# Graph layer on one core: the gathered-row step cut into five turns of five fours instead of six of four, with the PSUM banks shared out anew

## The chip, the core and the metric

The kernel runs on one core of one Trainium2 chip. The core has a matmul engine (PE, with its weight loads shown as PEld), a vector engine (DVE), an activation engine (ACT), a general engine (POOL), a queue engine (SP) and 16 DMA engines. PE writes only to PSUM, which has eight banks of 512 fp32 columns for each of 128 partitions; DVE and ACT read PSUM and read and write SBUF. The metric is device time of one execution in microseconds (us), lower being better.

## The reference

There are 12,500 nodes with 128 features and 400,000 edges, sorted by destination, each of one of two types. Every edge takes its source node's row through one of two linear maps, the results are summed at the destination, a self map is added, then relu, the residual and a layer norm:

```python
Xs = X[src]
m_data = Xs @ W_data.T + b_data
m_ctrl = Xs @ W_control.T + b_control
msg = jnp.where((edge_types == 0)[:, None], m_data, m_ctrl)
agg = jax.ops.segment_sum(msg, dst, num_segments=X.shape[0])
out = jax.nn.relu(agg + (X @ W_self.T + b_self))
return _layernorm(X + out)
```

Since the maps are linear, the kernel sums source rows for each destination and type first and multiplies by the weights once per node, in `finish_batch`.

## The kernel before

**Windows.** The edges are cut into 25 groups; a group holds five "p" windows and five "e" windows (the last e window of every odd group is joined to the p window before it). The main loop has 113 steps, one for each e window of 20 columns of 128 edges. A p window has 5 columns (25 where it is joined), which are spread over the steps, some eight columns a step.

**Rows of p windows** are gathered from memory: POOL issues an indirect DMA for each column (`fetch`, L743), and `chunk` sums them with three matmuls for the rows, which are held as three bf16 parts (L694), and one for the counts (L779).

**Rows of e windows** are picked on PE from node rows that stay in SBUF (`x3`). All edges of a window are sorted by source block ("cell") and rank beforehand, and a 0/1 matrix `pick` makes a matmul choose rows. Four cells make a "four", which is one bank of PSUM: four matmuls with 32 columns of weights each, side by side in four lanes of the array (`pick`, L808). There are 24 fours and half a one in a step, and edges that fit in no cell go to the tile `last`, gathered by POOL (L787).

**A step** (`picked`) has units. A unit first picks its fours into PSUM (`rows`, tile `got`), two fours to a tile, and ACT casts each tile of two banks to bf16 in SBUF (L820, tile `emsg`). Then it counts (L832) and adds (L694) the fours of the unit before it: a selection `esel` (edge against destination, made by DVE in `choose`, L500) is multiplied with the messages and summed into a bank of `sums`. The last unit's fours are added in `end`, which runs in the first unit of the next step, and then DVE adds the bank into `acc` (`accumulate`, L732).

**PSUM.** `ps1` has one bank, `side`, used for many short things in turn; `ps2` has three banks for `sums`, which e and p windows share; `psg` has two tiles of two banks for `got`. Together that is eight.

**Ranks for the window two steps on** are worked out in the same step: PE counts who stands ahead (L575, L516), DVE reduces and multiplies (L585 to L600), builds the value matrix (L626), PE puts values into cells (`put`, L638, in `side`), ACT copies them (`spread`, L646), SP writes them to memory and loads them back to all partitions as `pick` (L648, L650), DVE compares (L680), and PE turns the codes (`turn_codes`, L658, from ACT's copy). `O` (L500) and `prod` (L567, L568) of the next window are made in between.

**Order.** The code is recorded in the order in which `merged` sorts units by their place in the step (0 to 1): the units of `picked` lie evenly, the others at places that are written out, and a scheduler then places each engine's instructions by what it takes to be ready. Every engine runs its own queue in that order, and pools of tiles give the waits: a new tile waits until the last reader of the buffer that it takes is done. `paced` ties POOL's gathers to the picks of a unit.

Of the kernel before, what the change touches and what calls it, by code (L numbers as in the profile page):

```python
# [17 lines left out]
P = 128  # L18
D = 128
# [131 lines left out]
def short_path(ctx, tc, const, ident, eps, wT, brow, bad, x, src, dst, etype, ws, bs, out):  # L151
# [9 lines left out]
    ps2 = ctx.enter_context(tc.tile_pool(name="ps2", bufs=3, space=PSUM))  # L161
    psg = ctx.enter_context(tc.tile_pool(name="psg", bufs=2, space=PSUM))
# [379 lines left out]
    def give_slots(w):  # L542
# [39 lines left out]
        def ranks():  # L582
# [10 lines left out]
            half = big.tile([P, EC, h], BF, name="half")  # L593
# [69 lines left out]
        def keep_codes():  # L663
# [128 lines left out]
    def picked(w, tiled, ending, fin_used, before):  # L792
# [5 lines left out]
        per, pair = 4, 2  # L798

        def choose(q0, n=8):  # L800
# [13 lines left out]
        def rows(q):  # L814
            ps = psg.tile([P, pair, 512], FP, name="got")
            msg = two.tile([P, pair, 3 * D], BF, name="emsg", bufs=5)
            for k in range(pair):
                last = pick(ps[:, k, :3 * D], q + k)
                s["msg"][q + k] = msg[:, k, :]
            nc.scalar.copy(msg, ps[:, :, :3 * D])  # L820
            return last

        def last_rows():
            q = NQ - 1
            ps = psg.tile([P, pair, 512], FP, name="got")[:, 0] if fin_used else side()
            pick(ps[:, :3 * D], q, 2)
            nc.scalar.copy(s["msg"][q][OVF:, :], ps[OVF:, :3 * D])
# [13 lines left out]
        def unit(t):  # L841

            if t == 1 and w > 0:
                spare.append(lambda: spare_rows(w))
            for q in range(t * per, (t + 1) * per, pair):
                gate = rows(q)
            paced(w + (t + 1) / turns, gate)
            if t % 2:
                paced(w + (t + 1) / turns, gate)
            else:  # L850
                paced(w + (t - 1.5) / turns, gate)
            if t in (0, 1):
                choose(8 * t)
            if t == 0:
                ending()
            if t == 2:
                assert not spare
                s["msg"][NQ - 1] = slots[w]["last"]
            if t == 3:
                choose(16, 9)  # L860
            if t > 0:
                for q in range((t - 1) * per, t * per if t < turns - 1 else NQ):
                    count(q)
            if t == turns - 2:
                last_rows()
            if t == 1 and before:
                before()
            if t > 0:
                add((t - 1) * per, t * per)
# [12 lines left out]
        turns = (NQ - 1) // per  # L882
# [96 lines left out]
    def last_spares():  # L979
# [7 lines left out]
        return {6: [lambda: None, turn, s[3]]}, [(0.1, s[0]), (0.28, s[1])]  # L987
# [44 lines left out]
    def ending():  # L1032
        pass

    for w in range(pairs):
# [16 lines left out]
        units, ending = picked(w, tiled, ending, bool(rest), begin.pop(0)[1] if begin else None)  # L1052
# [181 lines left out]
```

## Time and profile before

| | before |
|---|---|
| median of 3 runs | 2022.85 us (2015.96 to 2024.19) |
| profiled execution | 2019.71 us, its span 2018.0 us |
| granted TensorE clock, mean | 0.993 |
| PE busy | 1758.2 us, 87% |
| DVE busy | 1654.6 us, 82% |
| ACT busy | 1318.0 us, 65% |
| POOL busy | 1222.2 us, 61% |
| casts of picked rows (L820) | 1356, 800 ns each |
| picks (L808 into `got`) | 10896, from 66.6 to 1993.2 us |

A share of busy time is a mean over stages; the timeline shows start, length, engine, line, operation, the tile written and those read, how many instructions are merged in the row, and in brackets how long the engine was idle before it and what ended that. A row of groups has the count, the total and the mean in ns, then the idle time just before them. A row of waits names who waited for what, with the total, the times and the longest in us. The ends of matmuls in the records are modelled, not observed.

### The profile page before, as it was taken

How to read it: one execution, taken by the hardware profiler on the slowest of the kernel's cores; microseconds unless marked ns; L12 is line 12 of the kernel's file. 1: busy time of each engine (PE TensorE's matmuls, PEld its weight loads, DVE VectorE, ACT ScalarE, POOL GpSimd, SP SyncE). 2: the span in 40 equal slices, each digit the busy share in tenths (PEclk: the TensorE clock that was granted, in tenths of full speed). 3: DMA queues.
4: the chain of work that ended last, by engine and by line, in shares of the span. 5: the costliest groups of instructions: out<-in, count | busy, mean ns of one | idle time of the engine just before them, and what ended most of it. 6: DMA issues, size and time to landing. Idle time of an engine off the chain costs nothing.

```text
span 2018.0 us, 74125 instructions
## 1 busy us (share of the span) xinstructions
PE 1758.2 (87%) x30869; PEld 1352.0 (67%) x30869; DVE 1654.6 (82%) x4158; ACT 1318.0 (65%) x2577; POOL 1222.2 (61%) x995
## 2 busy tenths in 40 slices
PE   0688899899889898999998999988998898999996
PEld 0466677677667676766776776766777677776675
DVE  7978888788788787888888888888888888788872
ACT  4656666676666665666666676666666666666665
POOL 0466666666666656666666666656666666666660
PEclk9999999999999999999999999999999999999999
DMA  8644343343343343443443443443434334334331
GB/s 237 202 115 137 108 140 119 120 134 121 110 138 121 118 138 98 140 135 104 140 122 118 139 123 119 137 124 113 134 124 129 115 122 125 122 125 126 120 101 40
DMA packets 186525, 254.84 MB, mean 126 GB/s; under 512 B 85369, under 2 KB 152995, under 8 KB 183108
## 3 DMA queue, kind: packets, MB, share of 16 engines
q1 hardware_dynamic: 128418, 152.97, 23.2%
q0 software_dynamic: 45136, 90.65, 16.5%
q10 hardware_dynamic: 12626, 6.40, 1.1%
q8 instruction: 243, 3.98, 0.8%
q14 instruction: 102, 0.84, 0.1%
HBM read 231.89 MB, written 18.04 MB: 124 GB/s over the span
## 4 chain that ended last, share of the span: by engine, by line
PE 67%; ACT 11%; DVE 8%; issue 6%; DMA 5%; SPq 1%; another core or an unknown queue 1%; DVEq 0%; ACTq 0%
PE sums L694 28%; PE got L808 25%; ACT emsg L820 8%; DMA pick<-there 3%; PE side L638 3%; PE side L938 3%; PE sums L832 2%; PE side L808 2%; PE side L575 1%; DVE esel L500 1%; PE side L526 1%; PE sums L779 1%; PE side L658 1%; DVE prod L567 1%
## 5 line engine op out<-in xcount | busy, mean ns | idle before, releaser
L743 POOL DMA_INDIRECT msg<-rows,pidx x865 | 1107.8, 1281 | 516.4 <-PE got L808 315.8
L820 ACT CAST emsg<-got 128x768 bf16<-128x768 f32 x1356 | 1025.0, 800 | 380.4 <-PE got L808 236.4
L694 PE MATMUL sums<-esel,emsg 128*128 128x176 bf16 x8136 | 748.9, 240 | 7.6 <-issue 7.2
L808 PE MATMUL got<-x,pick 128*32 128x384 bf16 x10896 | 655.0, 331 | 111.9 <-ACT emsg L820 55.0
L694 PEld LDWEIGHTS <-emsg 128*128 128x128 bf16 x8136 | 593.1, 98 | 121.0 <-issue 101.3
L808 PEld LDWEIGHTS <-pick 128*32 128x32 bf16 x11074 | 260.2, 95 | 291.6 <-issue 190.5
L500 DVE TENSOR_TENSOR esel<-code_col,code 128x1408 bf16<-128x1408 bf16 x339 | 309.1, 912 | 17.6 <-PE sums L694 11.2
L787 POOL DMA_INDIRECT last<-rows,idx x113 | 110.7, 979 | 248.0 <-ACT emsg L820 150.8
L500 DVE TENSOR_TENSOR O<-cell_col,blk 128x2000 bf16<-128x2000 bf16 x113 | 135.4, 1198 | 139.8 <-PE got L808 115.6
L694 PE MATMUL sums<-psel,msg 128*128 128x48 bf16 x2595 | 182.7, 184 | 5.6 <-issue 4.8
L832 PE MATMUL sums<-esel,one_col 128*32 128x176 bf16 x2825 | 166.8, 240 | 6.1 <-DVE esel L500 3.6
L732 DVE TENSOR_TENSOR acc<-acc,sums 128x352 f32 (+2 forms) x238 | 101.8, 428 | 66.5 <-PE sums L694 32.6
L694 PEld LDWEIGHTS <-msg 128*128 128x128 bf16 x2595 | 146.3, 98 | 7.0 <-issue 6.9
L680 DVE TENSOR_SCALAR pick<-pick,lane_f 128x3200 bf16<-128x3200 bf16 x113 | 119.2, 1055 | 32.7 <-DMA pick<-there 27.1
L779 PE MATMUL sums<-psel,one_col 128*128 128x48 bf16 x865 | 144.5, 183 | 1.4 <-issue 1.2
L589 DVE TENSOR_TENSOR prod<-O,ahead 128x2000 bf16<-128x2000 bf16 x113 | 134.4, 1190 | 0.0
L638 PE MATMUL side<-rv,O 128*128 128x64 bf16 x2260 | 91.0, 195 | 34.6 <-DVE rv L626 29.5
L832 PEld LDWEIGHTS <-one_col 128*32 128x32 bf16 x2825 | 85.9, 97 | 44.2 <-issue 9.9
L638 PEld LDWEIGHTS <-O 128*128 128x128 bf16 x2260 | 83.8, 100 | 37.6 <-DVE rv L626 30.2
L646 ACT CAST cell<-side 128x64 bf16<-128x64 f32 x113 | 23.5, 208 | 114.5 <-PE got L808 89.3
L585 DVE TENSOR_REDUCE ahead<-side 128x100 bf16<-128x500 f32 x113 | 76.3, 675 | 23.7 <-PE side L516 20.3
L626 DVE TENSOR_TENSOR rv<-rm,vals 128x1280 bf16<-128x1280 bf16 x113 | 92.2, 816 | 0.1
(172 smaller groups left out, 2008.8 us busy)
## 6 DMA issues: line engine op xcount, KB each, us to landing
pick<-there SPq DMA_DIRECT2D x113, 800.0 KB
acc<-acc_start SPq DMA_DIRECT2D x23, 1280.0 KB
msg<-rows,pidx POOLq DMA_INDIRECT x865
rows<-x SPq DMA_DIRECT2D x6, 1344.0 KB
xs<-in_x_dram SPq DMA_DIRECT2D x99, 62.5 KB
out_dram<-h SPq DMA_DIRECT2D x99, 62.5 KB
xt<-in_x_dram ACTq DMA_DIRECT2D x6, 896.0 KB
there<-cell SPq DMA_DIRECT2D x113, 6.2 KB
```

The lines of the kernel that those rows point to most:

```text
L500: nc.vector.tensor_tensor(sel.rearrange("p n (w t) -> p n w t", t=2), col[:rows].rearrange("p (o w t) -> p o w t", o=1, t=2).to_broadcast( ...
L589: nc.vector.tensor_tensor(prod, s["O"], ahead.rearrange("p (o j) -> p o j", o=1).to_broadcast([P, EC, NCELL]), op=OP.mult)
L638: nc.tensor.matmul(s["rk"][:m, :2 * CAP], s["held"][:, c * NCELL:c * NCELL + m], s["rv"][:, c].rearrange("p v r -> p (v r)"), start=(c == ...
L680: nc.vector.tensor_scalar(t, t, lane_f, None, op0=OP.is_equal)
L694: nc.tensor.matmul(out, msg[:, j * D:(j + 1) * D], sel, start=(start and j == 0), stop=stop, skip_group_check=True)
L732: added.append(nc.vector.tensor_add(win, win, ps[:, :4 * wide].rearrange("p (a w) -> p a w", w=wide)[:, :, :width]))
L743: return nc.gpsimd.indirect_dma_start(out=msg, out_offset=None, in_=rows3[:, :], in_offset=bass.IndirectOffsetOnAxis(ap=codes["p", g][0][: ...
L779: nc.tensor.matmul(cnt, one_col, sel, start=False, stop=(c == n - 1), skip_group_check=True)
L787: return nc.gpsimd.indirect_dma_start(out=msg[:OVF, :], out_offset=None, in_=rows3[:, :], in_offset=bass.IndirectOffsetOnAxis(ap=slots[w][ ...
L808: last = nc.tensor.matmul(ps[CAP * a:CAP * (a + 1), :], slots[w]["pick"][:, a * NQ + q, :], x3[:, 4 * q + a - a0].rearrange("p j d -> p (j ...
L820: nc.scalar.copy(msg, ps[:, :, :3 * D])
L832: nc.tensor.matmul(cells_of(s["ps"], EW, 1)[CAP * (q % 4):CAP * (q % 4 + 1), :], one_col[:, :CAP], s["sel"][q], start=(q < 4), stop=(q + 4 ...
```

## The change

- A step has five units ("turns") instead of six. They take fours 0 to 4, 5 to 9, 10 to 14, 15 to 18 with the half four, and 19 to 23 (`bounds`).
- A unit fills two tiles of `got`: one of two banks (`got2`) and one of three (`got3`), each with one buffer (`psg` has bufs=1). ACT casts two banks and then three at once; where the half four lies in the third bank (unit 3), it casts two and then the half. The messages have two tiles in two buffers each instead of one in five.
- The half four no longer has a bank of its own in `side` or `got` (`last_rows` goes, and with it `fin_used`).
- `sums` has two banks instead of three, so that five, two and one are again eight.
- The selections of a step are 10, 9 and 6 columns wide instead of 8, 8 and 9.
- The counts of the last unit's fours move from the last unit into `end`, ahead of `turn_codes`.
- Both gathers that `paced` may issue in a unit look at the end of the unit; before, the second of every other unit looked further back.
- `put` and `spread` go from unit 5 to unit 4, the last one in both, and `turn_codes` from 6 to 5. `ranks`, `over_matrix` and `rank_matrix` go from places 0.26, 0.28 and 0.3 to 0.31, 0.33 and 0.35, still just behind unit 1.
- The halves of the rank sums are written into the first half of `prod` instead of a tile of their own.

```diff
-    ps2 = ctx.enter_context(tc.tile_pool(name="ps2", bufs=3, space=PSUM))
-    psg = ctx.enter_context(tc.tile_pool(name="psg", bufs=2, space=PSUM))
+    ps2 = ctx.enter_context(tc.tile_pool(name="ps2", bufs=2, space=PSUM))
+    psg = ctx.enter_context(tc.tile_pool(name="psg", bufs=1, space=PSUM))
...
-            half = big.tile([P, EC, h], BF, name="half")
+            half = prod[:, :, :h]
...
-        s["tiled"] = {5: [put, spread], 6: [turn_codes, keep_codes]}
+        s["tiled"] = {4: [put, spread], 5: [turn_codes, keep_codes]}
...
-            (0.1, before), (0.26, ranks), (0.28, lambda: s["spares"][1]()), (0.3, rank_matrix), (0.75, over),
+            (0.1, before), (0.31, ranks), (0.33, lambda: s["spares"][1]()), (0.35, rank_matrix), (0.75, over),
...
-        per, pair = 4, 2
+        bounds = [0, 5, 10, 15, 19, NQ - 1]
+        turns = len(bounds) - 1
...
-            sel = select(sp.tile([P, 9, 2 * EW], BF, name="esel")[:, :n], code_col, slots[w]["code"][:, q0:q0 + n])
+            sel = select(sp.tile([P, 10, 2 * EW], BF, name="esel")[:, :n], code_col, slots[w]["code"][:, q0:q0 + n])
...
-        def rows(q):
-            ps = psg.tile([P, pair, 512], FP, name="got")
-            msg = two.tile([P, pair, 3 * D], BF, name="emsg", bufs=5)
-            for k in range(pair):
+        def rows(q, n, room, half=False):
+            ps = psg.tile([P, room, 512], FP, name=f"got{room}")
+            msg = two.tile([P, room, 3 * D], BF, name=f"emsg{room}")
+            for k in range(n):
                 last = pick(ps[:, k, :3 * D], q + k)
                 s["msg"][q + k] = msg[:, k, :]
-            nc.scalar.copy(msg, ps[:, :, :3 * D])
+            if half:
+                last = pick(ps[:, n, :3 * D], NQ - 1, 2)
+            nc.scalar.copy(msg[:, :n], ps[:, :n, :3 * D])
+            if half:
+                nc.scalar.copy(s["msg"][NQ - 1][OVF:, :], ps[OVF:, n, :3 * D])
             return last
-
-        def last_rows():
-            q = NQ - 1
-            ps = psg.tile([P, pair, 512], FP, name="got")[:, 0] if fin_used else side()
-            pick(ps[:, :3 * D], q, 2)
-            nc.scalar.copy(s["msg"][q][OVF:, :], ps[OVF:, :3 * D])
...
-            for q in range(t * per, (t + 1) * per, pair):
-                gate = rows(q)
-            paced(w + (t + 1) / turns, gate)
-            if t % 2:
-                paced(w + (t + 1) / turns, gate)
-            else:
-                paced(w + (t - 1.5) / turns, gate)
...
+            rows(bounds[t], 2, 2)
+            gate = rows(bounds[t] + 2, bounds[t + 1] - bounds[t] - 2, 3, t == 3)
+            for _ in range(2):
+                paced(w + (t + 1) / turns, gate)
...
         def end():
 
+            for q in range(bounds[turns - 1], NQ):
+                count(q)
             early, *more = tiled.get(turns, [lambda: None])
             early()
-            add((turns - 1) * per, NQ)
+            add(bounds[turns - 1], NQ)
...
-        return {6: [lambda: None, turn, s[3]]}, [(0.1, s[0]), (0.28, s[1])]
+        return {5: [lambda: None, turn, s[3]]}, [(0.1, s[0]), (0.33, s[1])]
```

More of the change, by code (lines that the diff above doesn't have):

```diff
@@ L844, in unit @@
                 spare.append(lambda: spare_rows(w))
[L845 to L856 removed]
+            if t == 3:
                 assert not spare
                 s["msg"][NQ - 1] = slots[w]["last"]
+            rows(bounds[t], 2, 2)
+            gate = rows(bounds[t] + 2, bounds[t + 1] - bounds[t] - 2, 3, t == 3)
+            for _ in range(2):
+                paced(w + (t + 1) / turns, gate)
+            if t == 0:
+                choose(0, 10)
+                ending()
+            if t == 1:
+                choose(10, 9)
             if t == 3:
[L860 removed]
+                choose(19, NQ - 19)
             if t > 0:
[L862 removed]
+                for q in range(bounds[t - 1], bounds[t]):
                     count(q)
[L864 to L865 removed]
             if t == 1 and before:
@@ L868, in unit @@
             if t > 0:
-                add((t - 1) * per, t * per)
+                add(bounds[t - 1], bounds[t])
             for u in tiled.get(t, []):
@@ L880, in end @@
             accumulate(g, 2 * i + 1, s["ps"], EW, EW)
-        turns = (NQ - 1) // per
         return evenly([lambda t=t: unit(t) for t in range(turns)]), end
@@ L1051, in short_path @@
             more += [(0.55, lambda: [u() for u in begin_slots(w + 3)])]
-        units, ending = picked(w, tiled, ending, bool(rest), begin.pop(0)[1] if begin else None)
+        units, ending = picked(w, tiled, ending, begin.pop(0)[1] if begin else None)
         merged(
```

4 lines of the change are left out of this document (2 added, 2 removed).

## The prediction

> **What bounds the kernel now.** I read the page's shares and its chain first, then the waits, the tile "got", the stretch of the steps, and one step engine by engine in the timeline.
>
> ```profile
> PE 1758.2 (87%) x30869; PEld 1352.0 (67%) x30869; DVE 1654.6 (82%) x4158; ACT 1318.0 (65%) x2577; POOL 1222.2 (61%) x995
> ...
> PE 67%; ACT 11%; DVE 8%; issue 6%; DMA 5%; SPq 1%; another core or an unknown queue 1%; DVEq 0%; ACTq 0%
> PE sums L694 28%; PE got L808 25%; ACT emsg L820 8%; DMA pick<-there 3%; PE side L638 3%; PE side L938 3%; PE sums L832 2%; PE side L808 2%; PE side L575 1%; DVE esel L500 1%; PE side L526 1%; PE sums L779 1%; PE side L658 1%; DVE prod L567 1%
> ```
>
> PE carries two thirds of the chain, but the cast of picked rows on ACT (L820), an engine only 65% busy, has 8% of it: PE waits for single casts, not for ACT's throughput. The waits of PE and the tile "got" say where:
>
> ```profile
> PE got L808 <- ACT emsg L820: 55.0, 174, 1.6
> PE got L808 <- issue: 44.5, 141, 1.1
> PE side L658 <- ACT cell L646: 41.1, 48, 4.1
> PE side L638 <- DVE rv L626: 29.5, 3, 18.1
> ```
> ```profile
> L808 PE MATMUL got<-x,pick x10896: 322/326/528, 66.6 to 1993.2; 128*32 128x384 bf16 x199
> ```
>
> From the first pick to the last are 1926.6 us, and 113 steps in them: 17.05 us a step, 2.84 us a unit of six and 3.41 us a unit of five. One of the quicker steps on PE, ACT and DVE (start, length, then what ended the idle time):
>
> ```profile
> 1002.80 0.39 PE L694 MATMUL sums<-esel,last 128*128 128x176 bf16 x3
> 1003.03 0.33 PE L526 MATMUL side<-bits_b,om_all 128*128 128x3 bf16 x7
> ...
> 1003.29 0.18 PE L779 MATMUL sums<-psel,one_col 128*128 128x48 bf16 x1
> 1003.40 0.83 PE L808 MATMUL got<-x,pick 128*32 128x384 bf16 x16
> 1004.07 0.25 PE L832 MATMUL sums<-esel,one_col 128*32 128x176 bf16 x4
> 1004.25 0.41 PE L575 MATMUL side<-prod,ltri 128*128 128x125 bf16 x4
> 1004.49 0.17 PE L516 MATMUL side<-over_n,ltri 128*128 128x1 bf16 x1
> ...
> 1005.62 0.83 PE L808 MATMUL got<-x,pick 128*32 128x384 bf16 x16
> ...
> 1007.88 0.51 PE L808 MATMUL got<-x,pick 128*32 128x384 bf16 x8
> 1008.66 0.51 PE L808 MATMUL got<-x,pick 128*32 128x384 bf16 x8 [0.27 <-ACT emsg L820]
> ...
> 1012.41 0.51 PE L808 MATMUL got<-x,pick 128*32 128x384 bf16 x8
> 1013.08 0.51 PE L808 MATMUL got<-x,pick 128*32 128x384 bf16 x8 [0.16 <-ACT emsg L820]
> 1013.40 0.39 PE L832 MATMUL sums<-esel,one_col 128*32 128x176 bf16 x9
> 1013.73 1.08 PE L694 MATMUL sums<-esel,emsg 128*128 128x176 bf16 x12
> 1014.65 0.77 PE L638 MATMUL side<-rv,O 128*128 128x64 bf16 x20
> ```
> ```profile
> 1007.03 1.58 ACT L820 CAST emsg<-got 128x768 bf16<-128x768 f32 x2 [1.47 <-PE got L808]
> 1008.77 1.50 ACT L820 CAST emsg<-got 128x768 bf16<-128x768 f32 x2 [0.16 <-PE got L808]
> ```
> ```profile
> 1003.23 0.52 DVE L732 TENSOR_TENSOR acc<-acc,sums 128x352 f32 x1 [0.54 <-PE sums L694]
> ...
> 1004.73 0.68 DVE L585 TENSOR_REDUCE ahead<-side 128x100 bf16<-128x500 f32 x1 [0.17 <-PE side L516]
> ...
> 1012.74 0.82 DVE L626 TENSOR_TENSOR rv<-rm,vals 128x1280 bf16<-128x1280 bf16 x1
> ```
>
> The reader is to see a ring: eight picks fill two banks, a cast empties them, and the picks of the next unit wait for that cast. The two casts of a unit take 1.58 us and begin 1.41 us after its picks (1005.62 to 1007.03), so they end 3 us after them, against a unit's mean of 2.84. The recorded idle time is too short: sixteen unbroken picks take 0.67 us to the next start (1003.40 to 1004.07), eight take 0.33. From 1007.88 to 1008.66 are 0.78, so 0.45 are lost where the row says 0.27; from 1012.41, 0.34 against 0.16. With 0.18 us more on each of 174 waits, 55.0 becomes 86 us.
>
> **The change, part by part.** All sums go against the profiled execution's own 2019.71 us (span 2018.0), 3 us under the median of the runs, 2022.85.
>
> *Units and pick banks.* Twelve casts of 768 a step become five of 768, four of 1152 and one of 768 (unit 3, where the half four rides in the third bank).
>
> ```profile
> L820 ACT CAST emsg<-got 128x768 bf16<-128x768 f32 x1356 | 1025.0, 800 | 380.4 <-PE got L808 236.4 <-PE side L808 52.0 <-PE sums L694 50.6
> L827 ACT CAST last<-side 64x384 bf16<-64x384 f32 x89 | 42.1, 473 | 3.5 <-PE got L808 1.2 <-PE sums L694 0.2
> ```
>
> No row shows a cast of 1152. From 384 columns at 473 ns and 768 at 800, 0.85 ns a column, it is 1127 ns; the bounds are that and 1200 (one and a half of the 800). I take 1.13. ACT does 9.79 us a step instead of 10.07, 32 us less in all, and none of it counts by itself, for ACT is not full. What counts is the ring: the second cast is 0.33 us longer, the unit 0.57 us on the mean and 0.48 in this quick step, whose turn of codes came 14.45 us before the next one's.
>
> ```profile
> 1001.75 0.20 PE L658 MATMUL side<-ident_b,cell 128*32 128x25 bf16 x4 [0.74 <-ACT cell L646]
> ...
> 1016.20 0.19 PE L658 MATMUL side<-ident_b,cell 128*32 128x25 bf16 x4
> ```
>
> Each wait shrinks by 0.15 to 0.24, say 0.2, from 86/174 = 0.49 to 0.29, and there are five sixths as many: 145 x 0.29 = 42. That saves about 40 us (bounds: 86 saved if all waits go; 33 lost, if each of the 145 grows by the 0.33 of the cast).
>
> *Turn of the codes.* L658 waits for ACT's copy of what L638 made. Now four more picks (0.17) and, since `end` counts before it turns, six counts (about 0.25, from 0.25 for four and 0.39 for nine) stand ahead of it: 0.41 us more cover for the 48 waits of 41.1 us, 0.86 each. I take 20 us off; 0 and 41 are the ends.
>
> *Counts.* The four lanes of counts run side by side. Groups of four, four, four, four and nine are seven rounds; five, five, five, four and six are nine. A round is (0.39 - 0.25)/2 = 0.07 us: 2 x 0.07 x 113 = 16 us more. One unit border less saves 0.11 us (1003.29 to 1003.40) less the 0.025 of an ordinary step: 10 us. Net 6 more.
>
> *Sums: three banks to two.* One holds the open e window, one the open p window, so each new window waits for DVE's L732 of a closed one. I count 236 such waits in the changed PE queue; behind each stand all of PE's picks. For e windows (111 of them) the last sum starts at 1002.95 (third of the row at 1002.80), and its L732 ends at 1003.75, 0.80 later; the counts come 1.12 us after it now and 1.28 with four more picks. Where DVE is on time it is free; for the times that it is late I take 5 us (ends 0 and 57, 0.5 us each). For p windows DVE is less prompt:
>
> ```profile
> 942.43 0.18 PE L779 MATMUL sums<-psel,one_col 128*128 128x48 bf16 x1
> ...
> 944.63 0.24 PE L694 MATMUL sums<-psel,msg 128*128 128x48 bf16 x3
> ...
> 1029.06 0.18 PE L779 MATMUL sums<-psel,one_col 128*128 128x48 bf16 x1
> ```
> ```profile
> 943.93 1.04 DVE L680 TENSOR_SCALAR pick<-pick,lane_f 128x3200 bf16<-128x3200 bf16 x1
> ...
> 945.30 0.31 DVE L732 TENSOR_TENSOR acc<-acc,sums 128x160 f32 x1
> ...
> 1029.28 0.66 DVE L732 TENSOR_TENSOR acc<-acc,sums 128x480 f32 x1
> ```
>
> That window closed at 942.4 and was added, behind L680 and others, only by 945.61; the next one's chunk started at 944.63 and would have waited 1.0 us. Another (closed at 1029.06, added from 1029.28) would have cost nothing. The changed PE order puts the first chunk a median of 2.2 us of unbroken PE work behind the last, some 2.6 with its stalls, against 3.2 and 0.9 in these two. One in two late by 0.4 is 0.2 us for each of 125 windows: 25 us (ends 0 and 125).
>
> *Half in place, and the order on DVE.* The three adds and the reduction keep their shapes, and the row of L595, in place today, has the same time for a column as L594's, so nothing; were it to cost, it is hidden by the slack below. The next window's L567 and L568 now stand behind L598, since they write what held the halves; nobody needs them before the next step.
>
> ```profile
> L594 DVE TENSOR_TENSOR half<-prod 128x1000 bf16<-128x1000 bf16 x113 | 76.3, 675 | 2.4
> L595 DVE TENSOR_TENSOR half<-half 128x480 bf16<-128x480 bf16 x113 | 45.5, 403 | 0.4
> ```
>
> The chain from L585 to L626 has 1.09 us to spare before L638 (1013.56 to 1014.65). L585 moves back by eight picks, five counts and three sums, 0.77 us, and forward by the 0.41 of the turn; the last selection shrinks from nine columns to six. That eats most of the slack, so some L638 will wait that don't now: 6 us (ends 0 and 57, half a us a step). Selections of 8, 8 and 9 columns become 10, 9 and 6: the same 25. SP issues the same transfers; POOL has ten chances a step to gather instead of twelve, for 8.7 gathers (865 and 113 in 113 steps): nothing, as long as the messages stay ahead.
>
> Sum: -40 - 20 + 6 + 5 + 25 + 6 = -18: 2001.7 us, 0.9% under this execution.
>
> **The rivals.** *The sums banks decide.* For it speaks the row at 945.30, against it the one at 1029.28. Without the p term the sum is 1977; at 0.5 us for each p window and 0.3 for each e window it is 2019.7 - 60 + 12 + 62 + 33 = 2067. From 0.34 us a p window on (43 us) the gain is gone. [...]
>
> *Longer casts hold PE longer.* If the late start of the cast, 1.4 us, and not its length, is what makes units long, and grows with the unit, each of 145 waits becomes 0.49 + 0.33 = 0.82, 119 us instead of 86. With the turn saved and the counts, e windows and L638 paid, and no p term, since PE then comes late to the sums anyway: 2019.7 + 33 - 20 + 17 = 2050. For it speaks the row at 1007.03, where ACT idled 1.47 us with picks recorded as done. [...]
>
> *One wait replaces the other.* PE that no longer waits for casts arrives earlier at the sums and at L638: gains of 60 and costs of 60 leave 2020.
>
> **How the numbers follow.** Forecast 0.46 (1975 to 2012 by itself); one wait for the other 0.18; sums banks 0.20; longer casts 0.16. About 0.5%, 10 us, is what a measurement can tell from no change: faster 0.46, same 0.18, slower 0.36. The range runs from 1962, gains near their bounds, to 2060, between the two slower rivals.
>
> **What will show it.** Right: PE's wait for the casts under 45 us, for L646 near 20; a cast of 1152 at 1.13 us; new rows "PE sums <- DVE acc" of some 30 us. Wrong: that row over 60, casts over 1.2 us, or L638 waiting for L626 in most steps.

## The result, and the profile after

The changed kernel takes 2045.32 us (median of 5 runs, 2041.25 to 2056.88) beside 2023.41 us for the kernel before: a ratio of 1.012, 95% interval 1.0096 to 1.0145. It is slower by 1.2% where 0.9% faster was forecast. The profiled execution took 2056.88 us, the longest of the five, so its 37 us over the profiled execution of before overstate the difference by some 15 us.

The page of the changed kernel, its shares and its chain, then the mean granted clock:

```profile
PE 1758.6 (86%) x30869; PEld 1387.2 (68%) x30869; DVE 1663.8 (81%) x4158; ACT 1300.5 (63%) x2351; POOL 1190.6 (58%) x995
...
PE 53%; DVE 15%; DMA 11%; issue 9%; ACT 8%; POOL 2%; another core or an unknown queue 1%; SPq 1%; DVEq 0%; ACTq 0%; POOLq 0%
```
```profile
core 0: 2054.9 us, clock 0.987
```

PE's busy time is what it was (1758.2 before), so by the records all of the added span is time in which PE stands: 2018.0 - 1758.2 = 260 us before, 296 us after. In the chain PE fell from 67% to 53%, while DVE rose from 8% to 15% and DMA from 5% to 11%. The waits of the changed kernel say which:

```profile
DVE pick L680 <- DMA pick<-there: 60.5, 39, 4.3
PE side L638 <- DVE rv L626: 53.1, 22, 18.2
PE got L809 <- ACT emsg L823: 34.8, 73, 0.9
DVE pick L680 <- issue: 29.9, 13, 4.4
PE sums L694 <- DVE acc L732: 26.1, 23, 3.9
PE got L809 <- ACT last L825: 20.2, 33, 1.0
PE side L658 <- ACT cell L646: 13.9, 7, 7.8
```

The turn of codes waits 13.9 us (41.1 before), 7.8 of them once, and the wait for the casts fell from 55.0 to 34.8 us, but the half four's own cast (L825) holds the picks for 20.2. New is that the sums wait for L732, that L638 waits for L626 22 times and not 3, and that DVE stands far longer ahead of L680. Two of L638's waits, some 28.9 us together, lie ahead of the steps in both kernels; in the steps themselves it waits 24.2 us in 20 of them, where it waited 0.7 us in one. DVE stands 90 us ahead of L680, the sum of its two rows above; the kernel before had these two, which the prediction did not use:

```profile
DVE pick L680 <- DMA pick<-there: 27.1, 31, 2.7
DVE pick L680 <- issue: 4.9, 3, 2.8
```

One step of the changed kernel shows how these belong together, on DVE, PE and SP in turn:

```profile
446.52 0.67 DVE L594 TENSOR_TENSOR prod<-prod 128x1000 bf16<-128x1000 bf16 x1
447.23 0.41 DVE L595 TENSOR_TENSOR prod<-prod 128x480 bf16<-128x480 bf16 x1
447.92 0.37 DVE L596 TENSOR_TENSOR prod<-prod,eq 128x400 bf16<-128x400 bf16 x1 [0.28 <-DVE prod L595]
452.59 1.05 DVE L680 TENSOR_SCALAR pick<-pick,lane_f 128x3200 bf16<-128x3200 bf16 x1 [4.30 <-DMA pick<-there]
453.56 0.68 DVE L598 TENSOR_REDUCE found<-prod 128x20 f32<-128x520 bf16 x1
...
455.86 0.81 DVE L626 TENSOR_TENSOR rv<-rm,vals 128x1280 bf16<-128x1280 bf16 x1
```
```profile
453.36 1.08 PE L694 MATMUL sums<-esel,emsg 128*128 128x176 bf16 x12
456.72 0.78 PE L638 MATMUL side<-rv,O 128*128 128x64 bf16 x20 [2.28 <-DVE rv L626]
...
458.07 1.79 PE L809 MATMUL got<-x,pick 128*32 128x384 bf16 x20
```
```profile
444.06 1.30 SPq L650 DMA_DIRECT2D pick<-there  x1
```

DVE has finished L596 and could go on with L598, L600 and L626, on which L638 waits. Ahead of them stands L680, whose data were ordered at 444.06 and are there only at 452.59. L598 starts only behind it, at 453.56, so the rank chain stands 4.30 us, L626 ends at 456.67, and PE stands 2.28 us with all its picks behind L638. The next twenty picks take 1.58 us to the next start, at 459.65. The windows before and after L638 show why (PE busy first, then PEld, DVE, ACT and POOL, then the granted clock):

```profile
453.00:456.70 3.70, 1.45 (x28) 1.07 (x17) 3.70 (x9) 1.57 (x2) 2.08 (x2) 1.00 0.13 35
456.70:460.20 3.50, 3.31 (x59) 2.18 (x59) 3.47 (x12) 1.35 (x4) 0.05 (x1) 0.59 0.21 49
```

After the wait the granted clock is 0.50 for 3.4 us, from 457.34 on. Between 70 and 1975 us the trace's clock records hold 4 stretches at half the clock before, 20.5 us, and 13 after, 44.4 us; L638 or the sums stand for 1.7 to 3.9 us just ahead of eight of the 13. Ahead of the one shown PE stood 2.28 us and was busy for 1.45 of 3.70 us; what brings such a stretch on is not shown. At half the clock, 24 us more are worth at most 12 us.

In the order of DVE's instructions, L680 stood ahead of L598 in 59 of the 113 steps before (behind L594 in 58 of them), between L598 and L626 in 46 and behind L626 in 8. In the changed program it stands behind L589 in 50, L594 in 25, L595 in 26 and L596 in 10: ahead of L598 in 111. No line of the diff names it; the scheduler placed it anew. So the theories were: (2) the place of L680 costs what was lost; against it (1) the two sums banks, (3) the halves in place, (4) the half four's cast.

L680 was inside the chain from L585 to L626 before, too. What its earlier place does can be read from the traces step by step (111 steps, means in us; PE is the time from the end of L516 until PE is free for L638, the chain the time from the end of L516 to the end of L626, and a step is late where the chain is the longer of the two; L638 starts some 0.05 us after the end of L626; the last column takes DVE's stand ahead of L680 out of each late step):

| kernel | PE | chain | of it L680, busy and stand | selections | late steps | L638 late, us | without the stand, us |
|---|---|---|---|---|---|---|---|
| before | 11.40 | 9.21 | 0.95 and 0.28 | 0.93 | 1 | 0.6 | 0.0 |
| changed | 10.85 | 9.44 | 1.03 and 0.78 | 0.51 | 20 | 23.1 | 0.8 |

The chain is hardly longer on the mean, for a selection left it while L680's stand grew. But the stand comes in lumps, 2.3 us in the late steps and 0.4 in the others, and PE reaches L638 0.55 us sooner, so the lumps are no longer covered.

### The profile page after: what moved, and what is told of

Read it like the earlier page. It is cut to its first block, busy times and chain, and to the rows that moved or that the text cites. A ratio compares the mean times of both kernels' runs of the same rounds, so it can differ in the third digit from the quotient of the medians.

```text
span 2054.9 us, 73709 instructions
## 1 busy us (share of the span) xinstructions
PE 1758.6 (86%) x30869; PEld 1387.2 (68%) x30869; DVE 1663.8 (81%) x4158; ACT 1300.5 (63%) x2351; POOL 1190.6 (58%) x995
## 3 DMA queue, kind: packets, MB, share of 16 engines
q1 hardware_dynamic: 128418, 152.97, 23.1%
## 4 chain that ended last, share of the span: by engine, by line
PE 53%; DVE 15%; DMA 11%; issue 9%; ACT 8%; POOL 2%; another core or an unknown queue 1%; SPq 1%; DVEq 0%; ACTq 0%; POOLq 0%
PE sums L694 20%; PE got L809 20%; DMA pick<-there 7%; ACT emsg L823 6%; PE side L934 4%; PE sums L831 3%; PE side L638 2%; POOL msg L743 2%; DVE esel L500 1%; PE side L575 1%; DVE rv L626 1%; DVE found L598 1%; DMA acc<-acc_start 1%; DMA msg<-rows,pidx 1%; DVE prod L567 1%
## 5 line engine op out<-in xcount | busy, mean ns | idle before, releaser
L743 POOL DMA_INDIRECT msg<-rows,pidx x865 | 1056.2, 1221 | 605.9 <-PE got L809 414.8
L823 ACT CAST emsg<-got 128x768 bf16<-128x768 f32 x1130 | 1011.2, 928 | 449.7 <-PE got L809 413.7
L694 PE MATMUL sums<-esel,emsg 128*128 128x176 bf16 x8136 | 732.0, 241 | 9.4 <-issue 8.4
L809 PE MATMUL got<-x,pick 128*32 128x384 bf16 x11074 | 642.8, 333 | 97.1 <-ACT emsg L823 34.8
L694 PEld LDWEIGHTS <-emsg 128*128 128x128 bf16 x8136 | 602.3, 98 | 84.5 <-issue 42.2
L500 DVE TENSOR_TENSOR esel<-code_col,code 128x1760 bf16<-128x1760 bf16 x339 | 310.5, 916 | 38.4 <-PE sums L694 18.1
L787 POOL DMA_INDIRECT last<-rows,idx x113 | 130.7, 1157 | 227.3 <-ACT emsg L823 102.6
L831 PE MATMUL sums<-esel,one_col 128*32 128x176 bf16 x2825 | 212.9, 242 | 18.3 <-DVE acc L732 9.8
L680 DVE TENSOR_SCALAR pick<-pick,lane_f 128x3200 bf16<-128x3200 bf16 x113 | 120.3, 1065 | 90.6 <-DMA pick<-there 60.5
L732 DVE TENSOR_TENSOR acc<-acc,sums 128x160 f32 (+2 forms) x238 | 101.8, 428 | 110.9 <-PE got L809 37.1
L831 PEld LDWEIGHTS <-one_col 128*32 128x32 bf16 x2825 | 124.4, 97 | 87.6 <-issue 34.1
L638 PE MATMUL side<-rv,O 128*128 128x64 bf16 x2260 | 88.9, 196 | 53.4 <-DVE rv L626 53.1
L589 DVE TENSOR_TENSOR prod<-O,ahead 128x2000 bf16<-128x2000 bf16 x113 | 134.4, 1189 | 0.0
L638 PEld LDWEIGHTS <-O 128*128 128x128 bf16 x2260 | 84.2, 101 | 59.9 <-issue 29.7
L585 DVE TENSOR_REDUCE ahead<-side 128x100 bf16<-128x500 f32 x113 | 76.3, 675 | 42.3 <-PE side L516 32.6
L626 DVE TENSOR_TENSOR rv<-rm,vals 128x1280 bf16<-128x1280 bf16 x113 | 92.4, 817 | 0.0
L646 ACT CAST cell<-side 128x64 bf16<-128x64 f32 x113 | 24.0, 212 | 101.9 <-PE got L809 53.8
```

Source lines behind the costliest of these rows:

```text
L500: nc.vector.tensor_tensor(sel.rearrange("p n (w t) -> p n w t", t=2), col[:rows].rearrange("p (o w t) -> p o w t", o=1, t=2).to_broadcast( ...
L589: nc.vector.tensor_tensor(prod, s["O"], ahead.rearrange("p (o j) -> p o j", o=1).to_broadcast([P, EC, NCELL]), op=OP.mult)
L626: nc.vector.tensor_tensor(rv.rearrange("p c v (r t) -> p c v r t", t=2), rm.rearrange("p c (o r t) -> p c o r t", o=1, t=2).to_broadcast(s ...
L638: nc.tensor.matmul(s["rk"][:m, :2 * CAP], s["held"][:, c * NCELL:c * NCELL + m], s["rv"][:, c].rearrange("p v r -> p (v r)"), start=(c == ...
L680: nc.vector.tensor_scalar(t, t, lane_f, None, op0=OP.is_equal)
L694: nc.tensor.matmul(out, msg[:, j * D:(j + 1) * D], sel, start=(start and j == 0), stop=stop, skip_group_check=True)
```

## The experiments

Beside the first four and the last two kernels the kernel before took 1869 and 1863 us, beside the others 2022 to 2042. It is not the chip: chip 6 gave 1869 and 2022, chip 9 gave 2042 and 1863. Each ratio stands against the kernel before that ran beside it, and only ratios, or traces of one such level, are compared.

| kernel | before | this | ratio (95%) |
|---|---|---|---|
| b_sums2 | 1869.10 | 1880.97 | 1.0064 (1.0045 to 1.0083) |
| b_half | 1869.10 | 1884.42 | 1.0078 (1.0059 to 1.0098) |
| a_rank | 1869.10 | 1809.94 | 0.9673 (0.9654 to 0.9692) |
| a_four | 1869.10 | 1980.86 | 1.0605 (1.0578 to 1.0631) |
| after_2 | 2042.33 | 2063.38 | 1.0099 (1.0065 to 1.0132) |
| b_rank | 2042.33 | 2049.92 | 1.0040 (1.0022 to 1.0057) |
| a_rank_2 | 2042.33 | 2041.04 | 0.9992 (0.9974 to 1.0011) |
| after_3 | 2041.75 | 2063.07 | 1.0112 (1.0075 to 1.0149) |
| b_sums2_2 | 2041.75 | 2057.89 | 1.0081 (1.0049 to 1.0112) |
| b_half_2 | 2041.75 | 2051.65 | 1.0047 (1.0031 to 1.0062) |
| a_pair | 2041.75 | 2039.76 | 0.9989 (0.9972 to 1.0006) |
| b_turn | 2022.12 | 2017.37 | 0.9975 (0.9955 to 0.9996) |
| a_own0 | 2022.12 | 2038.28 | 1.0080 (1.0057 to 1.0102) |
| a_own2 | 2022.12 | 2036.49 | 1.0074 (1.0051 to 1.0097) |
| a_rank_3 | 2022.12 | 2012.26 | 0.9961 (0.9942 to 0.9980) |
| a_calm | 1863.35 | 1928.25 | 1.0347 (1.0320 to 1.0374) |
| after_4 | 1863.35 | 1931.38 | 1.0367 (1.0326 to 1.0407) |

**The hold on L680 in the changed kernel** (a_rank, a_rank_2, a_rank_3). An ordering edge keeps L680 behind L600. The scheduler then puts it behind L626 in nearly all steps; lines from it on move by two (L682, L696, L734, L811).

```diff
-            nc.vector.tensor_copy(rank, found.rearrange("p (c o) -> p c o", o=1).to_broadcast([P, EC, 2]))
+            s["ranked"] = nc.vector.tensor_copy(rank, found.rearrange("p (c o) -> p c o", o=1).to_broadcast([P, EC, 2]))
...
-            nc.vector.tensor_scalar(t, t, lane_f, None, op0=OP.is_equal)
+            behind = slots.get(w + 1, {}).get("ranked")
+            with tc.issue_after(behind.ins) if behind else ExitStack():
+                nc.vector.tensor_scalar(t, t, lane_f, None, op0=OP.is_equal)
```

> The changed kernel with DVE's comparison L680 held behind the rank copy L600 of the same step, so that its wait for the pick DMA no longer stands ahead of the rank chain. Theory 2: L638's wait for L626 falls from 53 us to under 30, DVE's wait for the pick DMA from 60 to under 30, and the time to about 2020 to 2030. Theory 1: PE's waits for L732 stay near 26 us or grow, and the time stays within 8 us of the changed kernel's 2045. If the picks of the next step then come too late, a wait of PE's picks for L680 appears and the time rises over 2050.

> The changed kernel with L680 held behind L600, once more, beside the changed kernel itself. Theory 2: 3% under the kernel before and 4 to 5% under the changed kernel, DVE's wait for the pick DMA near 5 us. Theory 1 (sums banks): PE's waits for L732 near 27 us here as in the changed kernel, so they can't tell the two apart.

> The changed kernel once more, as the control beside the kernels below, since the runs of the experiments so far came from a chip on which the kernel before took 1869 us and not 2023. Theory 2 (the place of L680 on DVE): a ratio to the kernel before of 1.01 to 1.03, L638's wait for L626 and DVE's wait for the pick DMA both near 50 to 60 us. If the ratio is below 0.99 here, what the result showed depends on the chip, and the place of L680 explains less than the 3% that its move gave.

> The changed kernel as the control of a_calm on the same chip: 1.01 where the kernel before takes some 2020 to 2040 us; where it takes some 1870, the changed kernel was not measured, and the hold's 0.967 lets theory 2 expect 0.99 to 1.03.

One and the same edit takes the changed kernel from 1.0099 to 0.9992 where both ran side by side (2063.38 to 2041.04 us, 22 us), and from 1.0367 to 0.9673 across the two groups of runs where the kernel before takes under 1870 us, some 7%. That is more than the whole loss in both, so L680's place is enough to account for it, as theory 2 says. It is also more than an undoing: L680 leaves the chain, in which it was before the change as well, and the chain falls to 7.70 us in a_rank_2, from 9.48 in after_2 and 9.29 in before_2. The edge moves other instructions too; a selection that stood ahead of L598 goes behind L626 in 51 steps. Of what leaves the chain, L680 and its stand are 1.75 us a step, the selections 0.26.

The control after_3 gave 1.0112, as expected; other expectations were missed in size: a_rank_2 was to be 3% under the kernel before and was level with it, and after_4 lies above the 1.03 that it was to reach at most. Where the loss is large its rows are too; waits and clock of after_4:

```profile
PE side L638 <- DVE rv L626: 84.4, 42, 18.2
DVE pick L680 <- DMA pick<-there: 82.6, 47, 4.4
...
PE sums L694 <- DVE acc L732: 53.2, 38, 4.1
```
```profile
core 0: 1935.4 us, clock 0.972
```

and the same of a_rank, with the hold, and its row of L682 (of L638's waits 28.9 us lie ahead of the steps in both):

```profile
PE side L638 <- DVE rv L626: 31.2, 12, 18.2
PE sums L696 <- DVE acc L734: 27.4, 41, 1.5
```
```profile
L682 DVE TENSOR_SCALAR pick<-pick,lane_f 128x3200 bf16<-128x3200 bf16 x113 | 118.0, 1044 | 4.9 <-DMA pick<-there 4.8
```
```profile
core 0: 1808.6 us, clock 0.997
```

So 55.5 us of L638's waits in the steps become 2.3. The sums' wait for L732 is 27.4 us, half of after_4's 53.2 but about the 26 that theory 1 named, and the kernel is the fastest all the same.

**The trace of the kernel before beside it, and the control again.**

> The kernel before once more, for its trace beside those of the experiments. Theory 2: DVE's wait for the pick DMA near 30 us, L638's wait for L626 near 30 us. Theory 1: no wait of PE's sums for L732; that wait is then the whole of what two banks add, 27 to 36 us in the runs so far.

> The changed kernel as the control beside the three below. On a chip where the kernel before takes some 2030 us: a ratio of 1.01, as twice before. On one where it takes some 1870 us, where the changed kernel was not run yet and the hold on L680 gave 0.967: theory 2 expects 0.99 to 1.03 there, that is 2 to 6% over the kernel with the hold; if it is below 0.98, the hold does little there.

PE's groups between 70 and 1975 us give the idle time ahead of each, first before_2, then after_2, then a_rank_2, which ran side by side:

```profile
L808 PE MATMUL got<-x,pick 128*32 128x384 bf16 x10593 | 639.5, 331 | 129.5 <-ACT emsg L820 61.9 <-issue 56.6 <-ACT last L827 1.7
L694 PE MATMUL sums<-psel,msg 128*128 128x48 bf16 x2526 | 178.0, 184 | 7.9 <-issue 7.8
L832 PE MATMUL sums<-esel,one_col 128*32 128x176 bf16 x2750 | 161.9, 240 | 4.9 <-DVE esel L500 2.6 <-issue 2.3
L638 PE MATMUL side<-rv,O 128*128 128x64 bf16 x2200 | 88.1, 195 | 6.0 <-issue 4.8 <-DVE rv L626 1.0
...
L658 PE MATMUL side<-ident_b,cell 128*32 128x25 bf16 x440 | 22.1, 186 | 32.8 <-ACT cell L646 31.2 <-ACT h L968 0.7 <-issue 0.2
```
```profile
L809 PE MATMUL got<-x,pick 128*32 128x384 bf16 x10682 | 623.2, 332 | 101.6 <-issue 36.9 <-ACT emsg L823 33.7 <-ACT last L825 24.2
L831 PE MATMUL sums<-esel,one_col 128*32 128x176 bf16 x2719 | 204.9, 241 | 17.3 <-DVE acc L732 8.7 <-issue 7.5
L694 PE MATMUL sums<-psel,msg 128*128 128x48 bf16 x2499 | 170.0, 184 | 33.7 <-DVE acc L732 23.3 <-issue 8.7 <-DVE worst L436 1.1
L638 PE MATMUL side<-rv,O 128*128 128x64 bf16 x2160 | 84.1, 194 | 17.2 <-DVE rv L626 12.1 <-issue 2.4 <-DVE prod L568 2.2
...
L658 PE MATMUL side<-ident_b,cell 128*32 128x25 bf16 x432 | 28.8, 183 | 5.1 <-ACT cell L646 2.1 <-issue 1.7 <-ACT cnt L912 0.3
```
```profile
L811 PE MATMUL got<-x,pick 128*32 128x384 bf16 x10840 | 650.2, 331 | 118.5 <-issue 44.9 <-ACT last L827 33.8 <-ACT emsg L825 32.3
...
L696 PE MATMUL sums<-psel,msg 128*128 128x48 bf16 x2535 | 171.1, 184 | 14.9 <-DVE acc L734 10.7 <-issue 3.8
...
L638 PE MATMUL side<-rv,O 128*128 128x64 bf16 x2200 | 86.5, 194 | 3.2 <-issue 1.7 <-ACT pcol L446 0.6 <-DVE h L945 0.4
```

From before_2 to after_2 PE's picks gain 28 us and L658 gains 28; the p windows' sums lose 26, the counts 12, L638 11 and the finishing of nodes and smaller groups together some 25. With the hold the sums' loss shrinks to 7 and L638's is gone: with the same two banks PE's wait for L732 falls from 23.3 to 10.7 us. About half of what looked like the price of two banks was thus DVE standing at L680. The trace of after_2 agrees: sums and counts wait 34.3 us for L732, and 15.1 of these came while DVE had worked without a break since an L680 at which it had stood (44.1 of 62.0 in after_4).

**The same hold in the kernel before** (b_rank), where it puts L680 behind `rm` in 79 steps, behind L626 in 22 and behind L600 in 10.

> The kernel before with the same hold on L680 (behind the rank copy L600 of its step) and nothing else. If the hold alone makes the gain of 3%, this is as fast as the changed kernel with the hold, a ratio of 0.97, and five turns are worth nothing. If the hold only undoes what the change did to DVE's order, it lies between 0.99 and 1.00, and the rest of the 3% is the five turns' own. DVE's wait for the pick DMA falls below 10 us either way.

1.0040, a little slower: this edge has no gain of its own there. It isn't the same cure, though: L680 stays ahead of L626 in 89 steps, where the edge takes it out of the chain in the changed kernel, and the kernel before had next to no late L638 to win back (0.9 us in before_2). A hold behind L626 in the kernel before was not run. So the changed kernel with the hold is worth 0.1 to 0.4% (a_rank_2, a_rank_3), and 3.3% where the picks are quick; how much of that is the five turns and how much L680 outside the chain is not shown.

**One part at a time in the kernel before.** Two sums banks (b_sums2, b_sums2_2), the halves in place (b_half, b_half_2), and the counts of the last unit ahead of the turn of codes (b_turn):

```diff
-    ps2 = ctx.enter_context(tc.tile_pool(name="ps2", bufs=3, space=PSUM))
+    ps2 = ctx.enter_context(tc.tile_pool(name="ps2", bufs=2, space=PSUM))
```
```diff
-            half = big.tile([P, EC, h], BF, name="half")
+            half = prod[:, :, :h]
```
```diff
-                for q in range((t - 1) * per, t * per if t < turns - 1 else NQ):
+                for q in range((t - 1) * per, t * per):
...
         def end():
 
+            for q in range((turns - 1) * per, NQ):
+                count(q)
```

> The kernel before with two sums banks in place of three and nothing else. Theory 1 (the sums banks cost what the change lost): new waits of PE's sums for DVE's L732 of 20 to 40 us, and a time 20 to 45 us over the kernel before, some 2050. Theory 2 (DVE's order: the comparison L680, which waits for the pick DMA, stands ahead of the rank chain, so that L638 waits for it): the order on DVE hardly changes here, so L638 keeps its wait of about 30 us and the time rises by no more than 10 us, to 2033 at most.

> The kernel before with two sums banks, once more. Theory 1 says that the banks carry the loss: 1.005 to 1.01, with 25 to 40 us of waits of PE's sums for L732. If it is below 1.003 on a chip where PE's picks are slow, PE comes to the sums late enough there and theory 1 is out.

> The kernel before with the halves of the rank sums written into prod and nothing else. Theory 3 (halves in place set the next window's L567 and L568 behind L598 and tie DVE up): slower by 10 to 20 us, L638's wait for L626 rises above 40 us. Theory 1 and the prediction: no change, within 5 us of the kernel before. Theory 2: L680 moves later here, in half the steps behind L626, so no slower and perhaps 5 to 10 us faster, with DVE's wait for the pick DMA under the 27 us of before.

> The kernel before with the halves in place, once more. Theory 3: 1.005 to 1.01 here too, with L658's wait for ACT's copy or L638's wait for L626 some 15 to 30 us over the kernel before. The prediction's step (no cost while the slack before L638 covers it): within 0.3%.

> The kernel before with the counts of the last unit's fours moved into the end of the step, ahead of the turn of codes, and nothing else. The prediction's step: the 33 to 41 us that PE's L658 waits for ACT's copy shrink by some 0.3 to 0.4 us a wait (five counts more ahead of it), 15 to 20 us off the waits, and 10 to 20 us off the time, a ratio of 0.990 to 0.995. If PE only waits later instead (for the casts, or for DVE), the time stays within 0.3%.

Two banks alone cost 0.6 and 0.8%. The wait is there in b_sums2 and all but absent in b_sums2_2, the first line below and the second, so in the second the time does not go by this row, and by what it goes stays open:

```profile
PE sums L694 <- DVE acc L732: 36.2, 37, 3.0
```
```profile
PE sums L694 <- DVE acc L732: 3.3, 6, 1.5
```

The halves in place cost 0.8 and 0.5% in the kernel before (L638's wait for L626 was 60.4 us in b_half, 32.4 in b_half_2, where L658's was 49.7). This does not part theory 3 from theory 2: other than expected, L680 went forward here too, ahead of L598 in 90 steps where the kernel before has 59, so the halves in place are one reason why the scheduler moved it. Without DVE's stand at L680 the 29.4 us by which L638 is late in the steps of b_half would be 1.8. In b_half_2 it is late by 3.3 us alone, so what costs 0.5% there stays open. The moved counts gain 0.25%, about 5 us, half of the least that was expected of them and within the 0.3% of "PE only waits later".

**Banks and turns** (a_pair, a_four). a_pair is a_rank with the half four beside one four in the tile of two, so that the tile of three is cast at once; a_four keeps five turns but has the banks of before, each unit in tiles of two, two and one.

```diff
-            rows(bounds[t], 2, 2)
-            gate = rows(bounds[t] + 2, bounds[t + 1] - bounds[t] - 2, 3, t == 3)
+            first = 1 if t == 3 else 2
+            rows(bounds[t], first, 2, t == 3)
+            gate = rows(bounds[t] + first, 3, 3)
```
```diff
-    ps2 = ctx.enter_context(tc.tile_pool(name="ps2", bufs=2, space=PSUM))
-    psg = ctx.enter_context(tc.tile_pool(name="psg", bufs=1, space=PSUM))
+    ps2 = ctx.enter_context(tc.tile_pool(name="ps2", bufs=3, space=PSUM))
+    psg = ctx.enter_context(tc.tile_pool(name="psg", bufs=2, space=PSUM))
...
-            gate = rows(bounds[t] + 2, bounds[t + 1] - bounds[t] - 2, 3, t == 3)
+            gate = rows(bounds[t] + 2, 2, 2)
+            if t == 3:
+                gate = rows_half()
+            else:
+                gate = rows(bounds[t] + 4, 1, 2)
```

> The changed kernel with the hold on L680 and, in unit 3, the half four as the second bank of the tile of two (one four and the half) instead of the third bank of the tile of three. Theory 4 (the half's own cast, L825 in the changed kernel, keeps the tile of three from the next picks): the picks' waits for that cast fall from 20 to 34 us to under 10, and the time is 5 to 15 us under the changed kernel with the hold, a ratio of 0.991 to 0.997 on a chip where that stood at 0.999. If the picks wait as long for the cast of the tile of two instead, it makes no difference.

> The changed kernel's five turns with the banks of the kernel before: three sums banks, and pick banks in two tiles of two (a unit fills two, two and one; the half four goes by itself). Theory 1: the waits of PE's sums for L732 go, and the time falls to 2010 to 2025. Theory 2: L680 stands on DVE where it does in the changed kernel, so the wait for the pick DMA stays near 60 us and L638's near 50, and the time stays at 2035 or above. The wait of the picks for casts goes back to some 50 us or more in both, since the two tiles take turns again.

a_pair: 0.9989, no different from a_rank_2's 0.9992. The wait for the half's cast fell as expected, and the other rose by as much; waits of a_pair:

```profile
PE got L811 <- ACT emsg L825: 51.1, 105, 0.8
...
PE got L811 <- ACT last L827: 13.3, 28, 0.7
```

64.4 us together, against 66.1 in a_rank_2 and 63.6 in before_2. Theory 4 falls, and with it the hope in five banks: at this level, all three cuts of the ring leave the same wait for casts. a_four is 6% slower, a miss for both theories. ACT has 18% of its chain against 5% in a_rank, so three tiles over two buffers most likely make the casts the bound; its time tells nothing of the sums banks. Its waits tell something: with three banks again PE's wait for L732 is gone, as theory 1 expected, and with L680 ahead of L598 in 111 steps L638 still waits 51.0 us, as theory 2 did. So L638's wait does not need the two banks, while the sums' wait does.

**A tile of its own for the halves in the changed kernel** (a_own0; a_own2 with L680 held behind L626). Selections of 9, 9 and 7 columns make the room.

```diff
-            half = prod[:, :, :h]
+            half = big.tile([P, EC, h], BF, name="half")
...
-                choose(0, 10)
+                choose(0, 9)
...
-                choose(10, 9)
+                choose(9, 9)
...
-                choose(19, NQ - 19)
+                choose(18, NQ - 18)
```

> The changed kernel with a tile of its own for the halves again (room made by selections of 9, 9 and 7 columns in place of 10, 9 and 6), and no hold on L680, which here stands behind L589 in 52 steps, behind L594 in 23 and behind L600 in 33. Theory 3 (the halves in place cost 0.5% by themselves): 1.005 to 1.007 where the changed kernel has 1.011. Theory 2: L680 still ahead of the rank chain in two of three steps, so most of the wait for the pick DMA stays, 35 us or more.

> As a_own0, with L680 held behind L626, where it also stands in nearly all steps of a_rank_3. If the costs add up (halves in place 0.5%), this is 0.993 to 0.996 where a_rank_3 has 0.999, and faster than both kernels. If the halves in place cost something only because of L680's place, it is as a_rank_3, within 0.3%.

> The changed kernel with L680 behind L600, as the control of a_own2 on the same chip: 0.999 where the kernel before takes some 2040 us, 0.967 where it takes some 1870.

a_own0 came out at 1.0080, near what theory 3 asked for, but L680 stands ahead of L598 in 76 steps there, which theory 2 allows as well. a_own2 came out at 1.0074, 1.1% behind a_rank_3 instead of ahead of it. So the prices don't add up, and a held L680 isn't enough by itself: L638 is late in one step of a_own2, and the kernel is slow all the same. It differs from a_rank_3 in the tile, the cut of the selections and the order that the scheduler made of them (selections take 0.75 us of its chain and 0.30 in a_rank_3). Its clock records hold 65 us at half clock, against 14 in a_rank_3; that can be worth 26 us, about the whole difference of 24. Why PE falls there is open.

**Why the pick DMA is late** (a_calm). The edge loads that SP issues right behind L650 in some steps wait for L680 instead.

```diff
-            load(g + 2, "e")
-            load(g + 2, "p")
+            more.append((0.61, lambda w=w, g=g: [load(g + 2, "e", slots[w + 1]["compared"]), load(g + 2, "p")]))
```

> The changed kernel without the hold, with the edge loads of a later group (L196, L197, L204) behind the comparison L680 of their step in place of right behind the pick DMA. L680 stands here behind L595 in 56 steps and behind L600 in 57, so half the steps still have it ahead of L598 and L626. If the lateness of the pick DMA is what costs, DVE's wait for it falls from 59 us to under 20, L638's wait for L626 to 30, and the time is 0.7 to 1.3% under the changed kernel, as with the hold. If the place of L680 costs whatever the DMA does (1.05 us of L680 itself ahead of L598), the time stays within 0.4% of the changed kernel.

A miss: 1.0347 beside 1.0367, and the wait did not fall (the lines stand six further down here, so L686 is L680). For the same reason the expectation misread the order: its L595 and L600 are L589 and L594, and L680 is ahead of L598 in 111 steps, not in half:

```profile
DVE pick L686 <- DMA pick<-there: 95.4, 48, 4.0
```

These loads are not what makes it late. Why it is late is open; what the traces show is how early DVE comes: in the changed kernel it reaches L680 3.9 us after SP orders the load in the steps where it then stands over 1 us, and 5.9 us in the others. In a_rank it comes 9.3 us after, and stands in two steps only. What took the loss away was to take L680 out of the chain.

The changed kernel with the hold is level with the fastest here or the fastest: 0.9673, 0.9992 and 0.9961 of the kernel before, and 1.1% under the changed kernel where both ran side by side.

## Why the prediction was wrong

- **What bounds the kernel** was read rightly only for where the casts hold PE. The row of L680's wait for the DMA, 27 us before, was passed over, and DVE's order was taken as it stood apart from L567 and L568.
- **The step that failed** is "Half in place, and the order on DVE": it took 1.09 us of slack before L638 from one quick step, let the chain keep its length in every step, and put 6 us on what would be lost. The slack was 2.19 us on the mean and fell to 1.42, but the changed order puts L680, with a stand of up to 4.4 us, ahead of L598 in 111 steps, and 20 steps came late by it. L638's wait rose by 24 us in the first pair (the kernel before and the changed one of the result) and by 11 in the second (before_2 and after_2), and the same standing still of DVE delays L732, on which the sums wait. Taking L680 out of the chain gave 22 us, and some 7% at the other level. The three adds themselves cost nothing, as forecast (L594 took 675 ns before and 673 after), though the rows of L594 and L595 do not have "the same time for a column", 0.68 and 0.84 ns.
- **Units and pick banks**, -40 us, failed as well, and it is why the hold does not bring the forecast 0.9%: the idle time of the picks fell by 28 in after_2 and by 11 in a_rank_2, which has no DVE trouble. The wait for casts itself, the half's among them, stayed: 55.0 us in both of the first pair, 63.6 and 66.1 in before_2 and a_rank_2. There are fewer waits (106 against 174 in the first pair), each longer (0.52 against 0.32 us), where "each wait shrinks by 0.15 to 0.24" was forecast. The cast of 1152 columns was sized well, 1121 ns on the mean.
- **Turn of the codes**, -20 us: 28 off the idle time, so right there, though the time gains less: moving the counts alone gave 5 us (b_turn).
- **Counts and e windows**, +6 and +5: 12 us of new idle time before the counts, 8.7 of them for L732.
- **Sums**, +25 for the p windows: 26, right in size by luck, for about half of it came from L680; with the hold 7.
- **Not in the sum:** the clock (up to 12 us in the first pair, 0.993 to 0.987), and some 25 us before the finishing of nodes and smaller groups.
- **The rivals.** "Longer casts" gave the nearest number, 2050, by luck: its 119 us of waits for casts did not come, they stayed at 55. "The sums banks decide" names a real wait, about half of whose length came from L680. None of the rivals was DVE's order.
- **The signs** that were named for a right forecast nearly all came: 34.8 us for the casts (under 45 was named), 13.9 for L646 (near 20), casts of 1.12 us (1.13), 26 us for the sums (some 30), and L638 waited 22 times, not in most steps. The time went the other way all the same: the first sign left out the half four's cast, and none watched DVE ahead of L680.

## What to carry to other kernels

Where a scheduler orders an engine, list that engine's order in both programs before costing an edit, and look above all at instructions that wait for a DMA: one that moves ahead of a chain puts its wait into it, 4.30 us in the step shown. Look at the single steps, for a mean hides this: here the chain grew by 0.2 us on the mean, and 20 steps of 111 were late. A new wait of PE for an engine is not yet the price of the buffers in between (with the same two banks PE's wait for L732 fell from 23.3 to 10.7 us under the hold); look at what that engine stood waiting for. Such an instruction can be tied behind the chain with one ordering edge, which was worth 1.1% here, and 7% where the picks were quicker. List the order again after that: the edge moved selections too, and in a_own2, with L680 held too, the gain was not there.

## What was not expected of the hardware

The same program (a_rank and a_rank_2) took 1809.94 and 2041.04 us in two groups of runs, at granted clocks of 0.997 and 0.994; a_rank_3, on the chip of a_rank, took 2012.26. Its picks, the first row in a_rank and the second in a_rank_2:

```profile
L811 PE MATMUL got<-x,pick 128*32 128x384 bf16 x11074 | 592.0, 329 | 12.7 <-ACT emsg L825 8.1
```
```profile
L811 PE MATMUL got<-x,pick 128*32 128x384 bf16 x11074 | 662.3, 331 | 118.5 <-issue 44.9
```

Of the 227 us between their spans, 161 lie between the start of one pick and the next: twenty picks take 0.67 us from first to last start in at least three of four units of a_rank, and over 1.3 us in a quarter of the units of a_rank_2, partly with nothing recorded that they wait for. Casts that found ACT idle started within 0.11 us of the recorded end of the picks that released them in three of four cases in the one and within 0.86 us in the other, which fits recorded ends that are too early there. Slower picks leave DVE more time: from L516's end PE is free for L638 after 10.96 us in after_2 and after 9.91 in after_4, while the chain takes 9.48 and 9.28, so that L638 is late in 21 steps and in 45. So the change lost 1.0 to 1.2% there and 3.7% here. What makes the picks slow is open.
